# Conditioned two-layer transformer on one core: the values of loop one behind a step's energies, a bias behind the power, and the junction and the MLP's columns in other slots

## The chip, the cores and the metric

The kernel runs on one core of one Trainium2 chip. A core has a matrix engine (PE, with its weight loads shown apart as PEld), a vector engine (DVE), an activation engine (ACT), a general engine (POOL) and a sync engine (SP) whose queue issues nearly all DMAs of this kernel. Each engine takes its instructions in order. The metric is the device time of one execution in microseconds; less is better.

## The reference

The input is 32 sequences of 128 tokens with 512 features and one condition vector of 512 for each sequence. Two layers follow each other:

```python
# layer 0: 16 heads of 32, softmax after the energies, divided by sqrt(D)
h   = gamma(w) * layernorm(x) + beta(w)
q, k, v = h @ Wqkv.T + bqkv
out = softmax(q k^T) / sqrt(D) @ v;  out = out @ Wp.T + bp
h1  = out + x;   x1 = (gamma(w) * layernorm(h1) + beta(w)) + h1
# layer 1: one head of 512, then an MLP of 4 * 512 with an exact gelu
h   = film(rmsnorm(x1), cond)
x2  = x1 + softmax(Q K^T / sqrt(D)) V @ proj_w + proj_b
out = x2 + gelu(film(rmsnorm(x2), cond) @ mlp_w1 + b1) @ mlp_w2 + b2
```

## The kernel before

Everything is float32. A large product is made of three passes with rounded operands: each operand is split into a high part (rounded by a copy) and a low part (what is left, by a subtraction), and high*high, high*low and low*high are added in PSUM (`mm3`, line 157). So each tensor that goes into a product costs a copy (mostly on ACT) and a subtraction (on DVE or POOL).

The work has three stages. The instructions of PE, DVE, ACT and POOL stand in the order in which the program writes them (`manual_schedule`); the order of SP's DMAs is left to the framework's scheduler, and a DMA in SP's queue that waits for its data or its buffer holds up the DMAs behind it.

**Loop one** (layer 0) has 32 steps. Step s handles four heads of a group of four sequences. On PE it goes through the energies of step s (`pse`, line 526, 16 small matmuls), the queries of step s+1 (`psq`, 12 calls of line 157), five of the twelve calls of the projection of an earlier sequence (`psp`), a transposition of the row maxima (`psm`, line 545, called by `maxima`), the other seven projection calls, the energies again in transposed form with the maxima subtracted (`pst`, lines 556 and 561), the keys of step s+1 (`psk`), the heads' outputs and sums (`pso`, `pss`, lines 581 and 586), and then, after the step's end, the values of a sequence of the next group (`psv`, `values0`). Around them stand:
- DVE: the maxima's reductions (line 538) and their split (539, 540), the un-interleaving copy of a transposed sequence (`merge`, line 395), the statistics and the normalization of the next sequence (`stats`, `norm`, lines 296 to 301 and 374), the low part of a finished sequence (`low`, 425), the projection's sum with its residual (`add`, 625), the second normalization of that (`first` and `second`, 639 and 644), and the division of the heads (593 to 595).
- ACT: the bias of the queries and keys (509), the copy of the transposed maxima `mT` (547), four scalings and one rounding of a sequence (`rest`, lines 412 and 421), a copy that prepares the next sequence's DMA transposition (`halves`, 386), four exponentials (568), and the logarithm and exponential of the heads' sums (591, 592).
- POOL: the bias row that is added to the residual (`End.bias`, line 610, after its load), the power -1/2 of a variance (line 308), the sum with the shift (640), and low parts of weights (855, 858) and of heads' outputs (598).

In steps 0 to 3 there is no projection; steps 28 to 31 have no values left to make, and small products of weights (`psvp`, line 686) stand there between a step's heads and the next step's energies.

**The junction** runs once: eleven products that end loop one's last four projections and begin layer 1 (K and V are three and four streams of group 0). **Loop two** has 8 groups of 4 sequences (g = 0 to 7). For each group the scores (`pss`, line 747) are followed by eight slots u: four K products of the next group, then four V products, with the transposed attention (`psaT`) and the outputs (`pso`, line 805 adds and stores them) between them. `Pipeline` objects place the parts of a sequence's preparation into slots: `pipe` for layer 1, `tokens` for the MLP. A sequence that starts at slot t loads two slots earlier, takes its statistics at t, its normalization and `halves` at t+1, its `merge` and `rest` at t+6. `at` lists the (g, u) at which the MLP's first eight sequences start. `Columns` makes the MLP's right-hand operands of two sequences at a time: three sums (lines 890 to 893, DVE), four rounded copies (`heads`, 905, ACT) and four subtractions (`tails`, line 909, two on POOL and two on DVE). In `mm_tile`, the PSUM pool of the projections and the V products, there are two banks, so a V or a projection waits until the one two before it has been read by DVE (lines 123 and 625).

**The MLP** follows in four parts n of eight sequences; its first half-part starts inside the last group of loop two (`hidden(0, 0)`, seven products around the last attention). `Columns` for parts 1 to 3 are made in the second half of the part before.

Of the kernel before, what the change touches and what calls it, by code (L numbers as in the profile page):

```python
# [16 lines left out]
B, N, D = 32, 128, 512  # L17
# [5 lines left out]
G = 4  # L23
NG = B // G
# [17 lines left out]
def cond_seq_kernel(ctx: ExitStack, tc, x, condT, wcond, w0, w1, wk1, wm1, wm2, cols, rows, out):  # L42
    nc = tc.nc
# [14 lines left out]
    def mm_tile(name):  # L58
        return ps_mm.tile([P, D], FP, tag="mm", name=name)
# [7 lines left out]
    def w_tile(name, dt=FR, shape=(P, KC, D)):  # L67
        return big.tile(list(shape), dt, tag="w", name=name)
# [56 lines left out]
    def w_pair(name):  # L125
        return w_tile(f"{name}h"), w_tile(f"{name}l")
# [17 lines left out]
    def sub(pair, *sl):  # L144
        return tuple(t[(slice(None), *sl)] for t in pair)
# [396 lines left out]
    def maxima(s):  # L542

        ps = e_bank(f"psm{s}")[:, :P]
        nc.tensor.transpose(ps, nmx.rearrange("p r j -> p (r j)"), ident)
        mT[s] = sm.tile([P, P], FR, tag="mT", name=f"mT{s}", bufs=2)
        nc.scalar.copy(mT[s], ps)
# [318 lines left out]
    def a_load(n, h):  # L866

        t = w_tile(f"A{n}{'hl'[h]}").rearrange("p c f -> p (c f)")[:, : NA * 2 * P]
        load(t.bitcast(FP), ad[n % FH, h])
        At.setdefault(n, []).append(t.rearrange("p (c k f) -> p c k f", c=NA, k=2))  # L870

    class Columns:
# [9 lines left out]
        def sums(self):  # L882
            n, i = self.n, self.i
            if i == 0:
                Bt[n] = [w_pair(f"B{n}{nm}") for nm in "xuv"]
                t = w_tile(f"B{n}y")
                Bt[n].append((t[:, :2], t[:, 2:]))
            r1, r2 = self.r
            t = d_tile(f"T{n}_{i}", FP, (P, 2 * KC, P))
            nc.vector.tensor_tensor(t[:, 0:2], r2[:, :2], r1[:, :2], ALU.subtract)  # L890
            nc.vector.tensor_tensor(t[:, 2:4], r2[:, 2:], r2[:, :2], ALU.subtract)
            nc.vector.tensor_tensor(t[:, 4:6], r2[:, 2:], t[:, 0:2], ALU.subtract)
            nc.vector.tensor_tensor(t[:, 6:8], t[:, 4:6], r1[:, 2:], ALU.subtract)
            self.parts = [
                (*(p[:, :, ts(i, P)] for p in pair), src, eng)
                for pair, src, eng in zip(
                    Bt[n],
                    (r1, t[:, :4], t[:, 4:], r2[:, 2:]),
                    (nc.gpsimd, nc.gpsimd, nc.vector, nc.vector),
                )  # L900
            ]

# [346 lines left out]
    with tc.manual_schedule(engines=ordered):  # L1249
        new, end = coming(0), None  # L1250
        staged = None
        for s in range(STEPS):
            q, k = qk0(s + 1) if s + 1 < STEPS else ([], [])
            energies(s)
            if s == 0:
                ready.rest()
                ready = None
            if ready:
                ready.merge()
            if end:  # L1260
                end.bias()
            run(q)
            if s == STEPS - 1:
                staged()
                staged = None
            projection = end.stream() if end else []
            run(projection[:5])
            maxima(s)
            if ready:
                ready.rest()  # L1270
            if new:
                new.stats()
                new.norm()
            if ready:
                ready.low()
            if end:
                run(projection[5:])
                end.add()
                end.first()
            elif staged:  # L1280
                staged()
                staged = None
            wn, wj = divmod(s - W_FIRST, W_STEPS)
            if s in (3, 4):
# [12 lines left out]
            if s == 0:  # L1297
                staged = extras[0]()
            if s < KC:
                split_w(W0["p"], raw["p"], s, nc.gpsimd)  # L1300
            coming_stage = extras[s + 1]() if s + 1 in extras else None
            run(k)
            if s == STEPS - 1:
                K = keys1(0)
                run(K[0])
            heads_out(s)
            ready, new = new, coming(s + 1) if s + 1 < STEPS else None
            end = End(s + 1 - G, s + 1 == STEPS) if s + 1 >= G else None
            if s + G < B:
                run(values0(s + G))  # L1310
            if staged:
                staged()
            staged = coming_stage
            if s == 2:
                later["mods"] = r_tile("mods")
            wn, wj = divmod(s + 1 - W_FIRST, W_STEPS)
            if 0 <= wn < KC and wj == 0:
                weights = Weights(wn)
            if s == STEPS - 2:
                l1_load()  # L1320
# [8 lines left out]
        for slot in (-11, -10):  # L1329
            pipe.made[slot] = begins[slot]()  # L1330
        V = values1(0)
        products = [K[1], K[2], 0, K[3], 1, V[0], 2, V[1], 3, V[2], V[3]]
        for u, stream in enumerate(products):
            pipe.start(u - 11)
            if u == 1:
# [15 lines left out]
            pipe.end(u - 11)  # L1351


        at = [(1, 5), (2, 5), (3, 5), (4, 1), (4, 5), (5, 1), (5, 3), (5, 5)]
        batches = [0, 1, 4, 5, 2, 6, 3, 7]
        columns, COLUMNS = {}, (1, 2, 4, 6)
        tokens = Pipeline(
            {2 * G * g + u: lambda b=b: Turned(2, b) for (g, u), b in zip(at, batches)}
        )
        for g in range(NG - 1):  # L1360
            K, V = keys1(g + 1), values1(g + 1)
            outs = []
            run(scores1(g))
            softmax1(g)
            for u in range(2 * G):
                slot = 2 * G * g + u
                for line in (pipe, tokens):
                    line.start(slot)
                if u - 1 in columns:
                    columns[u - 1].tails()  # L1370
                if u in columns:
                    columns[u].sums()
                if 0 < u <= G:
                    outs.append(Out(g * G + u - 1))
                late = ends[g] if g < G else None
                if late and u == 0:
                    late.take_up()
                if late and u == 2:
                    late.first()
                if late and u == 4:  # L1380
                    late.second()
                run(K[u] if u < G else V[u - G])
                if u == 0:
                    divided1(g)
# [8 lines left out]
                if u in columns:  # L1393
                    columns[u].heads()
                if g == NG - 2:
                    if u + 1 in COLUMNS:
                        columns[u + 1] = Columns(0, COLUMNS.index(u + 1))
                    if u == 6:
                        for h in range(2):
                            a_load(0, h)  # L1400


        g = NG - 1
# [7 lines left out]
        products, started = hidden(0, 0)  # L1411
        for j in range(3):
            run(products[j])
        divided1(g)
        run(products[3])
        turn1(g)
        for o in outs:
            o.bias()
        run(products[4])
        for f in (0, FH):  # L1420
            wb_piece(f)
        for i, o in enumerate(outs):
            run(o.stream())
            if i < 2:
                run(products[5 + i])
        row2 = load(r_tile("row2"), rows[R_B2].partition_broadcast(P))
        for q in (1, 3):
            wb_load(q)
# [74 lines left out]
```

## Time and profile before

| | |
|---|---|
| median of 3 runs (lowest, highest) | 1509.9 us (1506.1, 1510.19) |
| the profiled execution: its own time, its span | 1510.46 us, 1508.5 us |
| PE busy | 1478.3 us, 98% of the span |
| DVE, ACT, POOL busy | 1008.4, 760.5, 499.5 us |
| PE idle, by stretch: up to 120 us, 120 to 580, 580 to 900, after | 9.0, 3.3, 12.7, 0.0 us |

A busy PE is not PE at its peak: matmuls are pipelined, and an instruction that waits in the queue behind its weight load can count as busy. So the distance between the starts of neighbouring instructions is read beside the busy time. A call of line 157 starts 0.227 us after the one before it where nothing is in the way. Loop one lasts from about 62 to 592 us, the junction to 627, loop two to 860, the MLP to the end.

### The profile page before, as it was taken

How to read it: one execution, taken by the hardware profiler on the slowest of the kernel's cores; microseconds unless marked ns; L12 is line 12 of the kernel's file. 1: busy time of each engine (PE TensorE's matmuls, PEld its weight loads, DVE VectorE, ACT ScalarE, POOL GpSimd, SP SyncE). 2: the span in 40 equal slices, each digit the busy share in tenths (PEclk: the TensorE clock that was granted, in tenths of full speed). 3: DMA queues.
4: the chain of work that ended last, by engine and by line, in shares of the span. 5: the costliest groups of instructions: out<-in, count | busy, mean ns of one | idle time of the engine just before them, and what ended most of it. 6: DMA issues, size and time to landing. Idle time of an engine off the chain costs nothing.

```text
span 1508.5 us, 25450 instructions
## 1 busy us (share of the span) xinstructions
PE 1478.3 (98%) x9612; PEld 1155.3 (77%) x9612; DVE 1008.4 (67%) x1793; ACT 760.5 (50%) x1415; POOL 499.5 (33%) x440
## 2 busy tenths in 40 slices
PE   8999999999999999999999899999999999999998
PEld 3767776777777766787887788888888888888887
DVE  4656777777777667889997776665557555754342
ACT  1455655566555444666786354535454345523331
POOL 1213554445453243466555422230014000340000
PEclk9999999999999999999999999999999999999999
DMA  8245465664655335788885877937776666934550
GB/s 312 85 151 157 125 198 176 188 190 134 178 152 175 111 115 178 193 209 225 233 214 173 356 238 236 307 132 209 225 266 208 194 203 219 326 122 134 184 173 29
DMA packets 226578, 287.85 MB, mean 191 GB/s; under 512 B 107252, under 2 KB 138100, under 8 KB 224024
## 3 DMA queue, kind: packets, MB, share of 16 engines
q1 hardware_dynamic: 225448, 278.89, 59.8%
q10 hardware_dynamic: 1008, 7.34, 1.4%
q8 instruction: 75, 1.23, 0.3%
q14 instruction: 47, 0.39, 0.1%
HBM read 194.23 MB, written 72.55 MB: 177 GB/s over the span
## 4 chain that ended last, share of the span: by engine, by line
PE 81%; DVE 11%; ACT 3%; issue 2%; POOL 1%; DMA 1%; SPq 0%; POOLq 0%; DVEq 0%; ACTq 0%
PE acc L981 23%; PE psh L157 20%; PE psk L157 6%; PE psv L157 5%; PE psq L157 5%; PE psp L157 5%; PE psV L157 2%; PE pse L526 2%; PE pst L561 2%; PE pso L581 2%; PE pss L586 2%; PE psT L157 1%; DVE tn L395 1%; PE pss L747 1%; DVE stn L296 1%
## 5 line engine op out<-in xcount | busy, mean ns | idle before, releaser
L308 POOL TENSOR_TENSOR rn<-vn,neghalf 128x1 f32<-128x1 f32 x96 | 61.6, 642 | 438.9 <-DVE vn L306 336.6
L386 ACT COPY tn<-x 128x1024 uint16<-128x1024 uint16 x90 | 94.0, 1045 | 60.5 <-DVE x L372 48.4
L919 ACT ACTIVATE c<-c,col 128x512 f32<-128x512 f32 x64 | 46.4, 725 | 141.2 <-DVE c L944 86.0
L538 DVE TENSOR_REDUCE nm<-pse 128x4 f32<-128x512 f32 x128 | 79.4, 682 | 19.4 <-PE pse L526 19.4
L997 POOL TENSOR_TENSOR xe<-xe,row 128x512 f32<-128x512 f32 x32 | 46.5, 1484 | 123.8 <-DMA xe<-xs 123.7
L934 DVE TENSOR_TENSOR c<-psh,ca 128x512 f32<-128x512 f32 x32 | 22.1, 692 | 89.9 <-PE psh L157 84.3
L395 DVE COPY tn<-tn 128x1024 uint16<-128x1024 uint16 x90 | 77.0, 855 | 1.0 <-DMA tn<-tn 1.0
L644 DVE SCALAR_TENSOR_TENSOR xe<-te,re,xe 128x512 f32<-128x512 f32 x28 | 41.1, 1467 | 47.4 <-POOL xe L640 47.4
L296 DVE BATCH_NORM_STATS2 stn<-x 128x6 f32<-128x512 f32 x96 | 65.4, 682 | 5.3 <-DMA x<-in_x 5.2
L568 ACT ACTIVATE e<-pst 128x512 f32<-128x512 f32 x128 | 65.8, 599 | 2.6 <-PE pst L561 2.5
L412 ACT ACTIVATE tn<-tn,mods 128x128 f32<-128x128 f32 x128 | 52.5, 481 | 19.0 <-DVE tn L395 19.0
L308 POOL TENSOR_TENSOR re<-ve,neghalf 128x1 f32<-128x1 f32 x32 | 30.9, 966 | 88.7 <-DVE ve L301 88.7
L372 DVE TENSOR_SCALAR x<-x,rn 128x512 f32<-128x512 f32 x64 | 52.9, 827 | 10.1 <-POOL rn L308 9.0
L610 POOL TENSOR_TENSOR xe<-xe,row 128x512 f32<-128x512 f32 x32 | 42.3, 1323 | 47.7 <-DMA xe<-in_x 46.8
L509 ACT ACTIVATE qk<-psq,col 128x512 f32<-128x512 f32 x32 | 22.1, 690 | 69.7 <-PE psq L157 63.5
L947 DVE TENSOR_TENSOR ca<-psh,ca 128x512 f32<-128x512 f32 x32 | 22.1, 691 | 41.5 <-PE psh L157 41.5
L561 PE MATMUL pst<-qk 32*128 32x128 f32 x1024 | 46.2, 295 | 0.0
L798 POOL TENSOR_TENSOR xe<-xe,row 128x512 f32<-128x512 f32 x32 | 45.8, 1444 | 1.1 <-DMA xe<-xs 1.1
L919 ACT ACTIVATE cb<-cb,col 128x512 f32<-128x512 f32 x32 | 23.2, 725 | 43.1 <-DVE cb L948 43.1
L526 PEld LDWEIGHTS pse<-qk 32*128 32x128 f32 x1024 | 32.1, 186 | 14.2 <-issue 12.7
L412 ACT ACTIVATE tn<-tn,mod 128x128 f32<-128x128 f32 x104 | 42.9, 485 | 0.0
L593 DVE TENSOR_TENSOR pss<-pss,rs 128x512 f32<-128x512 f32 x32 | 22.3, 697 | 29.9 <-ACT rs L592 29.8
(1388 smaller groups left out, 4846.5 us busy)
## 6 DMA issues: line engine op xcount, KB each, us to landing
mod<-mod SPq DMA_DIRECT2D x34, 512.0 KB, 5.4
x<-xs SPq DMA_DIRECT2D x64, 256.0 KB, 3.8
xe<-xs SPq DMA_DIRECT2D x64, 256.0 KB, 3.2
ur<-ud SPq DMA_DIRECT2D x64, 256.0 KB, 4.2
xs<-xe SPq DMA_DIRECT2D x60, 256.0 KB, 2.6
x<-in_x SPq DMA_DIRECT2D x32, 256.0 KB, 3.8
xe<-in_x SPq DMA_DIRECT2D x32, 256.0 KB, 4.3
scw<-scw SPq DMA_DIRECT2D x32, 256.0 KB, 4.7
```

Source lines behind the costliest of these rows:

```text
L157: nc.tensor.matmul(st["ps"], *calls[j], start=(j == 0), stop=(j == n - 1))
L296: nc.vector.bn_stats(st, t)
L308: nc.gpsimd.tensor_tensor(r, v, neghalf, ALU.pow)
L386: nc.scalar.copy(halves.rearrange("p (e d) -> p e d", e=2), X.bitcast(U16).rearrange("p (d e) -> p e d", e=2),)
L395: nc.vector.tensor_copy(self.a.bitcast(U16).rearrange("p (f e) -> p e f", e=2), self.t.bitcast(U16).rearrange("p (e f) -> p e f", e=2),)
L412: nc.scalar.activation(dst[:, c], self.a[:, ts(c, P)], AF.Identity, bias=m[:, q + B : q + B + 1], scale=m[:, q : q + 1],)
L526: nc.tensor.matmul(banks[r][:, ts(i, P)], q[32 * r : 32 * r + 32, ts(i, P)], k[32 * r : 32 * r + 32, ts(i, P)], start=True, stop=True,)
L538: nc.vector.tensor_reduce(nm[:, r], chunks(banks[r]), AX.X, ALU.max, negate=True)
L561: nc.tensor.matmul(banks[r][:, ts(i, P)], k[rr, ts(i, P)], q[rr, ts(i, P)], start=False, stop=True,)
L568: nc.scalar.activation(e, banks[r], AF.Exp)
L919: nc.scalar.activation(t[nm], t[nm], AF.Gelu, bias=col[:, C_B1 + f : C_B1 + f + 1], scale=1.0)
L981: nc.tensor.matmul(accs[i], u[pa][:, ts(i, P)], wb[f // 4][pb][:, f % 4, :], start=(first and j == 0), stop=(last and j == len(PARTS) - 1),)
```

## The change

Five places are edited; what is computed stays the same.

- In loop one the values of step s+3 move from the end of step s-1 (before the energies of step s) to behind the energies of step s. The bias of the residual (`End.bias`, POOL) moves from before the queries to behind the next sequence's statistics and normalization, and so behind their power on POOL. Of the projection's twelve calls nine instead of five stand before the maxima, three behind. And `ready.rest()` (ACT, lines 412 and 421) is now called before `maxima(s)`, so that ACT copies `mT` after it, and not before.
- In the junction the third K stream moves before the first projection, and from there on projections and V streams alternate.
- In loop two the starts of the MLP's sequences move to a start every four slots (slots 13, 17, ... 41 instead of 13, 21, 29, 33, 37, 41, 43, 45), and the first four `Columns` to slots 48, 50, 52 and 53 (before 49, 50, 52 and 54), with their loads two slots ahead instead of one.
- All four subtractions of `Columns` go to DVE, in all four parts of the MLP.
- In the last group, one more MLP product stands before the transposition of the attention.

```diff
-                    (nc.gpsimd, nc.gpsimd, nc.vector, nc.vector),
+                    (nc.vector,) * 4,
...
-            if end:
-                end.bias()
+            if 0 < s <= B - G:
+                run(values0(s - 1 + G))
             run(q)
...
-            run(projection[:5])
-            maxima(s)
+            run(projection[:9])
             if ready:
                 ready.rest()
+            maxima(s)
             if new:
                 new.stats()
                 new.norm()
+            if end:
+                end.bias()
             if ready:
                 ready.low()
             if end:
-                run(projection[5:])
+                run(projection[9:])
...
-            if s + G < B:
-                run(values0(s + G))
...
-        products = [K[1], K[2], 0, K[3], 1, V[0], 2, V[1], 3, V[2], V[3]]
+        products = [K[1], K[2], K[3], 0, V[0], 1, V[1], 2, V[2], 3, V[3]]
...
-        at = [(1, 5), (2, 5), (3, 5), (4, 1), (4, 5), (5, 1), (5, 3), (5, 5)]
+        at = [(1, 5), (2, 1), (2, 5), (3, 1), (3, 5), (4, 1), (4, 5), (5, 1)]
...
-        columns, COLUMNS = {}, (1, 2, 4, 6)
+        columns, FIRST = {}, 2 * G * (NG - 2)
+        columns_at = {FIRST + u: i for i, u in enumerate((0, 2, 4, 5))}
...
-        run(products[3])
+        for j in (3, 4):
+            run(products[j])
         turn1(g)
         for o in outs:
             o.bias()
-        run(products[4])
+        run(products[5])
...
-            if i < 2:
-                run(products[5 + i])
+            if i == 0:
+                run(products[6])
```

More of the change, by code (lines that the diff above doesn't have):

```diff
@@ L1368, in cond_seq_kernel @@
                     line.start(slot)
[L1369 to L1372, printed above, removed]
+                if slot - 1 in columns:
+                    columns[slot - 1].tails()
+                if slot in columns:
+                    columns[slot].sums()
                 if 0 < u <= G:
@@ L1392, in cond_seq_kernel @@
                     line.end(slot)
[L1393 to L1400, printed above, removed]
+                if slot in columns:
+                    columns[slot].heads()
+                if slot + 2 in columns_at:
+                    columns[slot + 2] = Columns(0, columns_at[slot + 2])
+                if slot == FIRST + 6:
+                    for h in range(2):
+                        a_load(0, h)
         g = NG - 1
```

## The prediction

> **What bounds the kernel now.** I read the page first, then PE's waits, then timelines of the places where PE's starts stand apart.
>
> ```profile
> span 1508.5 us, 25450 instructions
> PE 1478.3 (98%) x9612; PEld 1155.3 (77%) x9612; DVE 1008.4 (67%) x1793; ACT 760.5 (50%) x1415; POOL 499.5 (33%) x440
> PE 81%; DVE 11%; ACT 3%; issue 2%; POOL 1%; DMA 1%; SPq 0%; POOLq 0%; DVEq 0%; ACTq 0%
> ...
> PE psV L157 <- DVE V L123: 8.4, 7, 4.9
> PE psp L157 <- DVE xe L625: 1.8, 1, 1.8
> ```
>
> (The last two are PE's waits: total, times, longest.) PE bounds the kernel; no matmul is removed, so the change can win only stalls and transitions, and lose by new stalls. Next a quiet step of loop one (step 21, period 16.23 us), timelines of PE, ACT and DVE:
>
> ```profile
> 416.23 0.39 PE L157 MATMUL psp<-w0ph,o4h 128*128 128x512 f32 x1
> 419.19 0.34 PE L556 MATMUL pst<-mT,pick 32*128 32x128 f32 x4
> ...
> 416.43 0.69 ACT L509 ACTIVATE qk<-psq,col 128x512 f32<-128x512 f32 x1 [2.38 <-PE psq L157]
> 417.68 0.27 ACT L547 CAST mT<-psm 128x128 fp32r<-128x128 f32 x1 [0.56 <-PE psm L545]
> 417.84 1.65 ACT L412 ACTIVATE tn<-tn,mod 128x128 f32<-128x128 f32 x4
> 419.52 0.62 ACT L421 CAST n_24h<-tn 128x512 fp32r<-128x512 f32 x1
> ...
> 416.29 0.75 DVE L395 COPY tn<-tn 128x1024 uint16<-128x1024 uint16 x1
> ```
>
> The projection starts 0.2 us before ACT takes the queries' bias; `mT` is ready 1.2 us before pst needs it. Step 8, where the step takes 18.41 us:
>
> ```profile
> 201.70 1.29 POOL L610 TENSOR_TENSOR xe<-xe,row 128x512 f32<-128x512 f32 x1 [5.44 <-DMA xe<-in_x]
> 202.95 0.55 POOL L308 TENSOR_TENSOR rn<-vn,neghalf 128x1 f32<-128x1 f32 x1
> ...
> 204.11 1.05 ACT L386 COPY tn<-x 128x1024 uint16<-128x1024 uint16 x1 [2.70 <-DVE x L374]
> ...
> 205.71 2.41 PE L581 MATMUL pso<-e,v 128*32 128x128 f32 x31 [0.67 <-ACT e L568]
> ```
>
> A late load holds the bias, this the power behind it on POOL, this DVE's normalization, this ACT's copy and the exponentials behind it, and these PE. Last, group 6 of loop two, and the junction:
>
> ```profile
> 820.95 1.51 DVE L890 TENSOR_TENSOR T<-hT,hT 128x256 f32<-128x256 f32 x1
> ...
> 822.14 1.47 POOL L909 TENSOR_TENSOR B0xl<-hT,B0xh 128x512 fp32r<-128x512 f32 x1
> ...
> 832.70 0.79 PE L157 MATMUL psV<-w1vph,n_28h 128*128 128x512 f32 x1 [4.90 <-DVE V L123]
> 833.29 0.63 PE L157 MATMUL psV<-w1vpl,n_28h 128*128 128x512 f32 x1
> ...
> 611.61 0.50 PE L157 MATMUL psp<-w0ph,o7h 128*128 128x512 f32 x1 [1.80 <-DVE xe L625]
> 613.60 0.63 PE L157 MATMUL psp<-w0pl,o7h 128*128 128x512 f32 x1
> ```
>
> While POOL subtracts, DVE's 0.42 us sums take 1.51; DVE then reaches a V's low part late, PE waits 4.9 us, and afterwards its calls stand 0.43 instead of 0.227 us apart.
>
> **The change, part by part.**
>
> *Quiet steps.* ACT's order becomes queries' bias, four scalings, rounding, `mT`. With p the projection's start: the bias starts p+0.20; back-to-back ACT rows overlap by about 0.11, so the scalings start p+0.77, the rounding p+2.45, `mT` p+2.98 to 3.25, and pst p+3.30 (step 0 shows 0.05 from `mT` to pst). Now pst is at p+2.96: a loss of 0.34. The scalings need the merge. From the heads' end h, the last row of DVE's division ends h+3.5; the reductions, now without a wait for the energies (0.56), take 2.48, the split 0.35, the merge 0.75, so it ends h+7.05, and ACT is ready at about h+7.4: 0.35 to spare. Against the loss: energies no longer cut the stretch of long matmuls. Starts 0.32 instead of 0.227 into them and 0.34 after them go: 0.19. What energies cost right behind the sums (`pss`) no row shows; pso to pss suggests -0.1 to +0.1 of a change, and a gain can't be excluded; I take 0. Net +0.15 (bounds -0.1 to +0.35) in 23 steps (5 to 26, 28): **+3.5** (-2.3 to +8).
>
> *Bias behind the power.* The starts of the energies give steps of 18.41 (8), 18.50 (10), 17.47 (14), 17.11 (11), 16.63 (13), 16.57 (18) against 16.23: 7.3 us over, and ten others 1.1 together, mostly where the bias on POOL stretched line 539 or 540 (0.17) to 0.9 to 1.2. All go except that in 8, 10 and 14 the projection's sum (625) is late next: its chain to the end of line 644 takes 5.9 us, so the division and the merge slip by 0.55, of which 0.35 is covered: 0.2 each. **-7.8** (-8.4 to -5). What the bias meets instead is the normalization (374), 0.55 now; line 372 took 1.51 where a bias started just before it. Then `halves` starts at p+3.5 and ends p+4.6, the exponentials need pst's end at p+4.9: covered; without that cover up to 1 us a step, inside rival B. The sum 625 comes at p+4.2 instead of 4.55, so line 644 is no later.
>
> *Other steps.* In 29 and 30 a `psvp` stands before the energies, DVE splits it first and the merge ends 5.29 after the energies' start: scalings 5.32, pst 7.85 instead of 6.91: 0.94 each, and 0.26 in 31 (pst 7.62): **+2.1** (0 to +2.8). Step 1 has no projection; pst is at p+1.4, and becomes p+3.30: **+1.9** (1.5 to 3.6). Steps 2 to 4 have other PE work there and gain the transitions (0.6); step 27 has no `rest` and loses its late maxima (0.6) and a transition (0.2): **-1.4** (-2 to 0).
>
> *Junction.* It holds 4.2 us of stalls. V streams between projections give each bank one stream more, but every bias now stands behind a power of its own slot, the first also behind `low`. From the rows: power of sequence 7 at 607.2, bias 607.8 to 609.0, sum 609.7, while the second projection could start at 606.5: a 3.2 us wait; then small ones, end at 628 instead of 627. **+1** (-3 to +4.7, with the clock).
>
> *Groups 2 to 4.* Each of groups 2 and 3 gets one more start and merge: statistics 1.23, normalization 0.48, merge 0.75 on DVE, which is busy 28.0 of their 30.5 us already (PE's own work is 28.4). The start fits into a gap of 1.1; the normalization pushes V's low part by 0.55, the merge the next softmax (slack 0.7) by 0.1 to 0.7. 0.55 + 1.2 + 0.6: **+2.4** (0 to +6, both bounds from DVE's sum, idle or not). Tokens leave group 5 and 6: ACT's and DVE's merges at slots 49 and 51 go. Loads on SP follow with two slots of lead.
>
> *Group 6.* It lasts 36.37 us; groups without stalls 28.4 to 28.65. With POOL quiet but for four biases, DVE has 16.4 us for columns (four sums of 0.42, subtractions of 0.68 and 0.42) and 8.2 for the rest: 24.6. Its worst backlog stands at slots 53 and 54, where V's low part is just in time; with biases 0.5 late. 29.0: **-7.4** (-8 to -5).
>
> *Last group.* PE waits 1.69 for the divided attention; one product (1.36) covers most and the biases on POOL, earlier now, no longer stretch line 761 (1.22): -1.8. But A0l stands on SP behind the store of the third output (its sum about 25.7 into group 6) and took 6.7 to land; needed at 32.4: +1. **-0.8** (-1.85 to +1).
>
> *The MLP.* 24 subtractions of 0.68 move to DVE, 176 of 350 us busy from 1160 on, beside PE with no idle after 900: 0 (to +1; DVE would have to be late by a stream of 2.7 us).
>
> Sum: 3.5 - 7.8 + 2.1 + 1.9 - 1.4 + 1 + 2.4 - 7.4 - 0.8 = -6.5; the profiled execution took 1510.46 (0.56 above the median), so 1504.0.
>
> *The clock.* Granted clock 0.5 follows the wait of 1.80 us at 611.6 (for 3.41 us, 1.7 lost) but not the one of 1.69. [...]
>
> **Rivals.**
> - B, the copied maxima bind loop one: slower. Place: reductions, merge, scalings, rounding, `mT`, pst, back to the heads. It decides once the merge is over 0.35 later than I have it, or energies behind pss save nothing. For it: no wait covers `mT` any more. Against: the reductions lose their 0.56 wait. At +0.65 a step instead of 0.15: 23 x 0.5 = 11.5 more, 1515.5.
> - C, DVE takes it all back: groups 2 and 3 are DVE-bound, two starved V's bring the clock down, the junction waits. Groups +6, junction +4.5, group 6 only -6: 1512 at worst, 1509 likely.
> - D, energies behind the heads are nearly free and the junction's alternation works: steps -0.1 (-5.8), junction -2.5 (-3.5 against mine): 1495 to 1498.
>
> **How the numbers follow.** 0.3% (4.5 us) is about what a measurement here can tell from no change; the bound is 1505.4 to 1514.4. Mine 0.55 (1500 to 1509; 0.40 faster, 0.15 same), B 0.14 (0.12 slower, 0.02 same), C 0.16 (0.13 same, 0.03 slower), D 0.15 faster: faster 0.55, same 0.30, slower 0.15. Range 1497 to 1512.5: leaves out half of D's lower end and most of B.
>
> **What would show it.** Quiet steps near 16.4, pst starting just after `mT` behind line 421; steps 8, 10, 14 within 0.3 of the others, line 374 near 1.5; group 6 below 30.5 with line 890 at 0.42; groups 2 and 3 at 31 to 33; a wait of psp for DVE's line 625 at the junction. Wrong if quiet steps leave 16.1 to 16.6, or if PE's clock falls in loop one.

## The result and the profile after

The changed kernel takes 1521.1 us (median of 6 runs, 1518.4 to 1524.0) against 1509.3 for the kernel before (6 runs beside them, 1505.2 to 1511.0). The ratio is 1.0084, 95% interval 1.0064 to 1.0104: slower by 0.8%, where 1504.0 was predicted and 1512.5 was the upper end of the range. The profiled execution took 1519.41 us with a span of 1517.6.

The first page lines of the kernel after, the busy time of each engine and the shares of the chain that ended last:

```profile
span 1517.6 us, 25448 instructions
PE 1470.5 (97%) x9612; PEld 1156.5 (76%) x9612; DVE 1021.5 (67%) x1825; ACT 763.3 (50%) x1415; POOL 449.2 (30%) x408
PE 72%; DVE 14%; ACT 6%; issue 3%; DMA 3%; POOL 2%; SPq 0%; DVEq 0%; POOLq 0%; ACTq 0%
```

PE does the same 9612 products, its share of the chain fell from 81% to 72%, POOL is lighter by 50 us and DVE heavier by 13. PE's waits (total, times, longest) name where the time went:

```profile
PE pst L556 <- ACT mT L547: 15.3, 28, 2.2
PE psV L157 <- DVE V L123: 7.4, 5, 4.7
PE psp L157 <- DVE xe L625: 3.6, 2, 2.5
PE psh L157 <- DVE ca L951: 3.6, 1, 3.6
...
PE psaT L785 <- ACT B0y L905: 2.8, 1, 2.8
```

The first stood once before (0.8 us in step 0) and now stands all over loop one; the fourth, at the MLP's start, and the fifth, in group 6, are new; the second existed before, but its longest moved from group 6 to group 3. The starts of the stages, from both traces, give where the 9.2 us between the spans (1508.48 and 1517.64) lie:

| stretch | before | after | difference | predicted |
|---|---|---|---|---|
| loop one, first to last energies | 516.13 | 517.03 | +0.90 | -1.7, with the line below |
| last energies to layer 1's first K | 9.16 | 9.38 | +0.22 | |
| junction, to the scores of group 0 | 39.64 | 40.96 | +1.32 | +1 |
| groups 0, 1 and 5 | 87.41 | 87.37 | -0.04 | 0 |
| groups 2, 3, 4 | 90.85 | 95.79 | +4.94 | +2.4 |
| group 6 | 36.37 | 33.34 | -3.03 | -7.4 |
| scores of the last group to the end | 666.88 | 671.76 | +4.88 | -0.8 |

A quiet step of loop one in the kernel after (step 21, 16.36 us), timelines of PE, ACT, DVE and POOL:

```profile
417.76 0.33 PE L556 MATMUL pst<-mT,pick 32*128 32x128 f32 x4 [0.28 <-ACT mT L547]
...
415.25 1.64 ACT L412 ACTIVATE tn<-tn,mod 128x128 f32<-128x128 f32 x4
416.92 0.62 ACT L421 CAST n_24h<-tn 128x512 fp32r<-128x512 f32 x1
417.45 0.26 ACT L547 CAST mT<-psm 128x128 fp32r<-128x128 f32 x1
...
416.47 1.50 DVE L374 TENSOR_SCALAR x<-x,mvn,rn 128x512 f32<-128x512 f32 x1 [0.66 <-POOL rn L308]
...
416.40 1.28 POOL L610 TENSOR_TENSOR xe<-xe,row 128x512 f32<-128x512 f32 x1
```

This is as predicted: pst starts right behind `mT`, which stands behind the rounding; the bias meets the normalization (1.50 instead of 0.55 us).

Group 6, where slot 48 now makes its column sums; timelines of DVE, ACT and PE:

```profile
817.39 1.22 DVE L761 TENSOR_TENSOR nm<-usn,nm 128x4 f32<-128x4 f32 x1
...
818.72 1.55 DVE L890 TENSOR_TENSOR T<-hT,hT 128x256 f32<-128x256 f32 x1
...
821.63 1.48 DVE L892 TENSOR_TENSOR T<-hT,T 128x256 f32<-128x256 f32 x1
823.14 0.42 DVE L893 TENSOR_TENSOR T<-T,hT 128x256 f32<-128x256 f32 x1
823.49 0.17 DVE L775 RECIPROCAL inv<-total 128x4 f32<-128x4 f32 x1
823.69 0.69 DVE L776 TENSOR_TENSOR e<-e,inv 128x512 f32<-128x512 f32 x1
...
824.13 0.40 ACT L905 CAST B0y<-hT 128x256 fp32r<-128x256 f32 x1
...
824.53 1.06 PE L785 MATMUL psaT<-ident,e 128*128 128x128 f32 x4 [2.80 <-ACT B0y L905]
```

The sums (0.42 us when POOL is quiet, as line 893 shows) stand between the softmax and the division of the attention (775 and 776) on DVE, and POOL's seven biases (line 798, 813.6 to 822.8) stretch three of them to 1.5. The row of `psaT` names ACT's last copy, which ends at the same moment; but `psaT` starts 0.15 us after the end of the division (824.38), and 0.14 after it in a kernel below where those copies come later, so the division is what PE waits for. The three biases beside the sums take 4.13 us, 1.38 each, hardly more than the 1.28 of a bias in loop one, while each of the three sums takes 1.5 instead of 0.42, 1.1 us longer: nearly all of the lost time stands in DVE's rows.

At the MLP's start (DVE and PE):

```profile
885.11 0.74 DVE L395 COPY tn<-tn 128x1024 uint16<-128x1024 uint16 x1 [7.10 <-DMA tn<-tn]
885.74 0.68 DVE L951 TENSOR_TENSOR ca<-psh,ca 128x512 f32<-128x512 f32 x1
...
886.47 0.79 PE L157 MATMUL psh<-B0vh,A2h 128*128 128x512 f32 x1 [3.56 <-DVE ca L951]
```

DVE waits 7.1 us for a transposition that a merge needs, and the sum of the seventh product, for which PE waits, stands behind the merge. In the kernel before the same merge waited too, and PE did not:

```profile
875.99 0.75 DVE L395 COPY tn<-tn 128x1024 uint16<-128x1024 uint16 x1 [1.05 <-DMA tn<-tn]
```

### The profile page after: what moved, and what is told of

It reads as the page before. It is cut to its first block, busy times and chain, and to the rows that moved or that the text cites. A ratio compares the mean times of both kernels' runs of the same rounds, so it can differ in the third digit from the quotient of the medians.

```text
span 1517.6 us, 25448 instructions
## 1 busy us (share of the span) xinstructions
PE 1470.5 (97%) x9612; PEld 1156.5 (76%) x9612; DVE 1021.5 (67%) x1825; ACT 763.3 (50%) x1415; POOL 449.2 (30%) x408
## 4 chain that ended last, share of the span: by engine, by line
PE 72%; DVE 14%; ACT 6%; issue 3%; DMA 3%; POOL 2%; SPq 0%; DVEq 0%; POOLq 0%; ACTq 0%
PE acc L981 21%; PE psh L157 19%; PE psk L157 6%; PE psv L157 5%; PE psq L157 5%; ACT tn L412 3%; PE pst L561 2%; PE pso L581 2%; PE psV L157 2%; PE pse L526 2%; DVE tn L395 2%; PE pss L586 2%; DVE stn L296 1%; PE psT L157 1%; DVE x L372 1%
## 5 line engine op out<-in xcount | busy, mean ns | idle before, releaser
L997 POOL TENSOR_TENSOR xe<-xe,row 128x512 f32<-128x512 f32 x32 | 44.3, 1410 | 191.8 <-DMA xe<-xs 175.7
L556 PE MATMUL pst<-mT,pick 32*128 32x128 f32 x512 | 40.5, 306 | 15.3 <-ACT mT L547 15.3
L798 POOL TENSOR_TENSOR xe<-xe,row 128x512 f32<-128x512 f32 x32 | 45.3, 1434 | 15.9 <-DMA xe<-xs 15.9
L556 PEld LDWEIGHTS pst<-mT,pick 32*128 32x128 f32 x512 | 25.0, 186 | 29.1 <-ACT mT L547 29.0
L374 DVE TENSOR_SCALAR x<-x,mvn,rn 128x512 f32<-128x512 f32 x26 | 35.2, 1352 | 17.6 <-POOL rn L308 17.6
```

The costliest lines, as they stand in the source:

```text
L556: nc.tensor.matmul(banks[r][:, ts(i, P)], pick[rr, i], mT[s][rr], start=True, stop=False)
```

## The experiments

"From psh to the end" is the time from the first product of the MLP to the end of the span (663.39 before, 668.27 after); the length of a group is that between the starts of two scores.

**Which half lost it.** First the four edits of loop one alone:

```diff
-            if end:
-                end.bias()
+            if 0 < s <= B - G:
+                run(values0(s - 1 + G))
             run(q)
...
-            run(projection[:5])
-            maxima(s)
+            run(projection[:9])
             if ready:
                 ready.rest()
+            maxima(s)
...
+            if end:
+                end.bias()
...
-            if s + G < B:
-                run(values0(s + G))
```

> Only the four edits of loop one (values, bias, the nine projection calls, scalings ahead of the maxima's copy); junction, loop two, columns and last group as before. Theory S (the loss lies in the second half): a quiet step of 16.38 us, layer 1's first K after loop one starts 1.7 us later than before, loop two and the MLP's start as before: +1 to +3 us, 1510 to 1513. Rival L (loop one's new order is the loss, and loop two's new stalls only follow from its shifted transfers): 1516 to 1521, with stalls of 3 to 5 us in loop two here too.

Measured: 1509.7 against 1510.0, ratio 1.0010 (0.9997 to 1.0023). The quiet steps take 16.34 to 16.40, the first to the last energies 519.29 us (516.13 before), and from the first K to the end nothing is lost. Of the 3.2 us, step 1 has 2.9 (a wait of 2.16 us and a half clock behind it, which the profile of after does not have). The profiled execution (1507.9) is not longer than that of the kernel before all the same, as it came to its first energies 3.7 us earlier (58.30 instead of 62.04 us after its start); the kernel after, with the same four edits, has 62.01 there. Theory S holds: these four edits lose nothing behind loop one.

Then all the other edits without these:

```diff
-        products = [K[1], K[2], 0, K[3], 1, V[0], 2, V[1], 3, V[2], V[3]]
+        products = [K[1], K[2], K[3], 0, V[0], 1, V[1], 2, V[2], 3, V[3]]
...
-        at = [(1, 5), (2, 5), (3, 5), (4, 1), (4, 5), (5, 1), (5, 3), (5, 5)]
+        at = [(1, 5), (2, 1), (2, 5), (3, 1), (3, 5), (4, 1), (4, 5), (5, 1)]
...
+        columns_at = {FIRST + u: i for i, u in enumerate((0, 2, 4, 5))}
...
-                    (nc.gpsimd, nc.gpsimd, nc.vector, nc.vector),
+                    (nc.vector,) * 4,
...
-        run(products[3])
+        for j in (3, 4):
+            run(products[j])
...
```

> Everything but loop one's four edits: junction, starts of the MLP's sequences, columns, subtractions on DVE, last group. Theory S: the stalls of group 3 (4.7), group 6 (2.8) and the MLP's start (3.6), each with half a clock for 3.4 us, are here too: group 6 3 us shorter, group 3 about 4.5 longer, the stretch behind the last scores about 5 longer: +6 to +8, 1516 to 1518. Rival L: the stalls come with loop one's shift and go here: group 6 alone is left, 1503 to 1508.

Measured: 1518.8, ratio 1.0068 (1.0050 to 1.0085); group 3 takes 36.01, group 6 33.35, and from psh to the end 667.65. All three stalls are there without any shift of loop one. The loss lies in these edits; rival L falls.

**The order of ACT in loop one.** The first kernel of this section without one of its four edits:

```diff
-            if ready:
-                ready.rest()
             maxima(s)
+            if ready:
+                ready.rest()
```

> The same without one edit: the scalings stand behind the maxima's copy again, as before the change. Theory S with the copy as the binding link of a quiet step: the copy is ready by itself, the 0.28 us wait of pst goes and steps take 16.05 to 16.15; steps 10, 11, 13 and 15 lose their waits of 0.5 to 1.6 too; layer 1's first K 6 to 10 us earlier than in the kernel with all four edits, time 1501 to 1506. Rival: the energies behind the sums, with the values behind them, make the maxima themselves late, whatever ACT does first: steps stay at 16.3 to 16.4 and the time within 2 us of the kernel with all four edits.

Measured: 1505.7, ratio 0.9968 (0.9953 to 0.9983): faster than the kernel before. First to last energies 512.33, 7.0 less than with the scalings first; the waits of pst for `mT` are gone but for step 0. Of the 7.0, step 1 gives 3.2 (its 2.16 us wait and the half clock behind it), steps 29 and 30 1.2, steps 10 to 15 3.0 and step 26 0.7, while steps 8 and 27 lose 0.9 and 1.1; the quiet steps 16 to 25 give only 0.05 each (16.30 to 16.32). The medians differ by 4.0 only: four kernels with the scalings first have the half clock of step 1 in their profile (17.9 us), three do not (16.34 to 16.40). The quiet steps are now held by something else. ACT and PE of that kernel in step 14, which takes 16.30 like them, then DVE and ACT in step 11, which takes 16.86:

```profile
297.00 1.04 ACT L386 COPY tn<-x 128x1024 uint16<-128x1024 uint16 x1
297.95 2.05 ACT L568 ACTIVATE e<-pst 128x512 f32<-128x512 f32 x4
...
300.84 0.27 PE L581 MATMUL pso<-e,v 128*32 128x128 f32 x1
```

```profile
245.78 1.49 DVE L374 TENSOR_SCALAR x<-x,mvn,rn 128x512 f32<-128x512 f32 x1 [0.67 <-POOL rn L308]
...
247.31 1.05 ACT L386 COPY tn<-x 128x1024 uint16<-128x1024 uint16 x1 [0.40 <-DVE x L374]
```

pst has ended at 296.8, but the copy of line 386 stands ahead of the exponentials, so that the last one comes late and the last output product (`pso`) slips in between the sums. Step 26, which has no such copy, takes 15.98. In step 11 the copy starts 0.53 us later in the step than in a quiet one (11.95 instead of 11.42 us after the first energies), behind a normalization that the bias beside it stretches to 1.49, and the step is 0.56 longer.

**Line 386 behind the exponentials.** (With the subtractions on DVE too, which is the next experiment; the base is that kernel.)

```diff
-            if new:
-                new.halves()
             exponentials(s)
+            if new:
+                new.halves()
```

> The same, and in loop one the copy that prepares the next sequence's transposition (line 386) stands behind the four exponentials on ACT instead of ahead of them. Theory E (with the maxima's copy first, the steps' remaining excess is the last exponential: the outputs wait for it 0.1 to 0.25 us in a quiet step and up to 0.9 in steps 8, 11, 13 and 15, where a normalization stretched by the bias holds that copy): quiet steps 16.04 to 16.15 instead of 16.30, steps 8 to 15 within 0.4 of them, 5 to 8 us faster than the kernel without this edit. Rival: the transposition goes out 3 us later, lands behind its place and the merge is late: steps of 16.3 or more, no gain or a loss.

Measured: 1520.8, ratio 1.0075 (1.0058 to 1.0092), against 1504.7 without this edit. (The profiled execution, 1512.8, was the fastest, so its rows hold half of the loss.) Undisturbed steps do take 15.98 to 16.12 (5 to 8, 16 to 18, 20, 22, 23, 25, 26), as theory E says, but steps 9 to 13 take 18.0 to 19.7 and others 16.8 to 17.4. In step 11 the timelines of ACT, PE and SP show:

```profile
245.18 0.62 ACT L597 CAST o2h<-rs 128x512 fp32r<-128x512 f32 x1 [6.92 <-DVE rs L595]
...
246.33 0.50 PE L157 MATMUL psp<-w0ph,o1h 128*128 128x512 f32 x1 [2.33 <-ACT v L493]
...
241.41 0.32 SPq L645 DMA_DIRECT2D xs<-xe  x1
241.82 1.30 SPq L390 DMA_TRANSPOSE tn<-tn  x1
```

The later transposition queues on SP behind a store that waits for line 644, and the next load behind the transposition; DVE's division comes late, and the values' copy, which stands behind the heads' rounding on ACT, holds the bank that the projection needs. Both theories had a part of it: an undisturbed step takes about 16.05, and with this order of the loads too many steps are disturbed.

**The bias alone.**

```diff
-            if end:
-                end.bias()
             run(q)
...
                 new.norm()
+            if end:
+                end.bias()
```

> One edit of loop one alone: the bias of the residual behind the power. By the prediction's term -7.8 us: steps 8, 10, 14, 11, 13 and 18 lose 7.3 us of their excess, 1501 to 1504. Rival (what the changed kernel shows in steps 10, 11, 13 and 15, 4 us over in all): the late load only hands its wait to the projection's sum and through DVE to the next step, and half of the gain goes: -3 to -4, 1505 to 1507.

Measured: 1506.9, ratio 0.9984 (0.9972 to 0.9996). Step 8 falls from 18.41 to 16.23 and step 18 from 16.57 to 16.22, but 10 stays at 18.44 (18.50) and 14 at 17.41 (17.47), and steps 9, 12, 13, 15, 29 and 30 become 0.2 to 0.6 longer (12: 16.79 instead of 16.23); first to last energies 513.93, 2.2 less instead of 7.8. The rival is right in its size, not in its cause. Step 10 on DVE in the kernel before, and then in this one on DVE and POOL, with SP's queue ahead of it:

```profile
235.25 0.69 DVE L296 BATCH_NORM_STATS2 stn<-x 128x6 f32<-128x512 f32 x1 [2.15 <-DMA x<-in_x]
...
238.39 0.55 DVE L374 TENSOR_SCALAR x<-x,mvn,rn 128x512 f32<-128x512 f32 x1 [2.04 <-POOL rn L308]
```

```profile
231.98 0.70 DVE L296 BATCH_NORM_STATS2 stn<-x 128x6 f32<-128x512 f32 x1 [2.50 <-DMA x<-in_x]
...
233.75 1.50 DVE L374 TENSOR_SCALAR x<-x,mvn,rn 128x512 f32<-128x512 f32 x1 [0.66 <-POOL rn L308]
...
233.68 1.29 POOL L610 TENSOR_TENSOR xe<-xe,row 128x512 f32<-128x512 f32 x1
...
223.30 0.34 SPq L645 DMA_DIRECT2D xs<-xe  x1
...
225.70 0.94 SPq L86 DMA_DIRECT2D x<-in_x  x1
```

The sequence's own load `x` is late as well as the one that the bias waits for. Both queue behind the store of line 645, and the statistics waited for `x` in the kernel before already. The edit lets the normalization start 1.02 us earlier in the step (9.03 instead of 10.05 us after the first energies). But the bias now starts beside it and stretches it from 0.55 to 1.50 us, so that it ends at 10.53 instead of 10.60, and the copy of line 386 and the exponentials behind it come no earlier. In step 12 it starts 0.31 us earlier and ends 0.62 later. A quiet step covers the longer normalization (it stays at 16.22); in step 8 the bias's load comes after the power, and the normalization keeps its 0.55. No run has the bias behind the normalization.

**Group 3.** Two edits of the changed kernel's starts, one slot earlier, and back to those of before:

```diff
-        at = [(1, 5), (2, 1), (2, 5), (3, 1), (3, 5), (4, 1), (4, 5), (5, 1)]
+        at = [(1, 5), (2, 0), (2, 5), (3, 0), (3, 5), (4, 0), (4, 5), (5, 0)]
```

> The changed kernel with the MLP's new starts one slot earlier ((2,0), (3,0), (4,0), (5,0) instead of (.,1)): as many statistics, merges and scalings on DVE and ACT in each group. Theory H (the divided attention's tile aT of group 3 gets the buffer of an MLP sequence whose store hTd was issued 5 us before and holds ACT 2.7 us; V's low part is late by that): the store goes out a slot (3.6 us) earlier, ACT does not wait, group 3 takes 30.5 to 31.5 us instead of 35.05, no half clock at its end. Rival D (DVE's sum of work makes group 3 late, as the prediction counted): 34 to 35 again.

```diff
-        at = [(1, 5), (2, 1), (2, 5), (3, 1), (3, 5), (4, 1), (4, 5), (5, 1)]
+        at = [(1, 5), (2, 5), (3, 5), (4, 1), (4, 5), (5, 1), (5, 3), (5, 5)]
```

> The changed kernel with the starts of the MLP's sequences of before. Both H and D: groups 2 and 3 as before, 30.5 each (-0.5 and -4.5). Group 6 gets the merges of slots 49 and 51 back: 33.3 if its stall is the columns' place alone, up to 36 if DVE's sum counts there. Behind the last scores as in the changed kernel (the loads' order is the changed one). 1515 to 1518 against 1519 to 1521.

Measured: one slot earlier 1524.1 (ratio 1.0103, 1.0073 to 1.0132), groups 2 and 3 32.60 and 34.70; the old starts 1514.8 (1.0041, 1.0021 to 1.0061), 30.49 and 30.49, with group 6 at 34.93, between the two lengths expected. So it is the new starts that lengthen groups 2 and 3. With the starts one slot earlier ACT has no wait of `aT` for a store any more, which was this in the kernel after:

```profile
ACT aT L122 <- DMA hTd<-tn: 2.7, 1, 2.7
```

but group 3 is hardly shorter (34.70 instead of 35.05) and group 2 is longer. Theory H falls as the cause of the length: it names only where the stall showed. What stays in each is DVE's work. The columns of these rows are the window, its length, busy time and instructions of PE, PEld, DVE, ACT and POOL, granted clock, DMA share and GB/s; groups 2 and 3 of before, of after, and of the starts one slot earlier:

```profile
685.72:716.23 30.51, 29.16 (x146) 24.08 (x145) 28.02 (x59) 21.80 (x47) 18.30 (x17) 1.00 0.86 233
716.23:746.75 30.52, 29.16 (x145) 24.07 (x144) 28.05 (x59) 21.79 (x47) 18.30 (x17) 1.00 0.90 244
```

```profile
688.10:719.16 31.06, 29.15 (x145) 24.08 (x144) 29.58 (x64) 22.82 (x48) 19.32 (x18) 1.00 0.95 243
719.16:754.21 35.05, 30.31 (x146) 25.07 (x144) 30.91 (x68) 25.26 (x54) 19.23 (x19) 0.95 0.91 236
```

```profile
690.03:722.63 32.60, 29.20 (x146) 24.00 (x144) 30.19 (x66) 23.21 (x49) 18.50 (x18) 1.00 0.86 225
722.63:757.33 34.70, 30.55 (x146) 25.19 (x145) 31.88 (x66) 24.52 (x53) 20.64 (x19) 0.95 0.90 237
```

DVE's busy time in the two groups goes up by 4.42 us (after) and 6.00 (one slot earlier); the two groups take 5.08 and 6.27 longer, about 1.7 of it in each by the half clock at the end of group 3 (3.41 us at 0.5). So rival D holds as to the length. That DVE's work makes it is argued from these sums: they agree over the two groups together and not in each (group 2 of after has 1.56 us more work and is 0.55 longer, group 3 2.86 and 4.53). How much of the 4.5 us of group 3 belongs to the wait of `aT` and how much to the sum was not separated.

**Group 6.** The changed kernel with the columns' slots of before:

```diff
-        columns, FIRST = {}, 2 * G * (NG - 2)
-        columns_at = {FIRST + u: i for i, u in enumerate((0, 2, 4, 5))}
+        columns, COLUMNS = {}, (1, 2, 4, 6)
...
```

> The changed kernel with the columns at slots 49, 50, 52 and 54 as before, all subtractions on DVE. Theory C (in the changed kernel the sums of slot 48 stand between the softmax and the division of the attention on DVE, under POOL's biases, and their copies ahead of psT's on ACT): the wait of 2.8 us and the half clock behind it go, group 6 takes 28.7 to 29.7 us instead of 33.33. Rival: POOL's biases stretch whatever DVE has there, 32 to 33.5. A3h and A3l stand behind the outputs' stores in this kernel: behind the last scores 5 us late as in the changed kernel, or more.

Measured: 1515.4 (1.0048, 1.0026 to 1.0070), group 6 30.17 at full clock. Theory C is right to within half a microsecond. DVE and PE in that kernel:

```profile
821.95 0.18 DVE L775 RECIPROCAL inv<-total 128x4 f32<-128x4 f32 x1 [1.64 <-ACT e L766]
...
823.23 0.41 DVE L890 TENSOR_TENSOR T<-hT,hT 128x256 f32<-128x256 f32 x1
...
823.45 0.63 PE L785 MATMUL psaT<-ident,e 128*128 128x128 f32 x4 [1.43 <-DVE e L776]
```

The sums stand behind the division, and POOL's biases are over by then (at 822.8). From psh to the end it takes 664.81, so the expected 5 us there did not come, which points at the next question.

And the other way round, the subtractions on DVE with the old slots and starts, on top of the loop with the maxima first:

```diff
-                    (nc.gpsimd, nc.gpsimd, nc.vector, nc.vector),
+                    (nc.vector,) * 4,
```

> Loop one as in the kernel with the maxima's copy first (values behind the energies, bias behind the power, nine calls, scalings behind the copy), and all four subtractions of the columns on DVE; junction, starts, the columns' slots and the last group as before. Against the kernel with the maxima first alone, 1505.7. Theory C (group 6 was held by POOL's subtractions alone; DVE's sum there is 24.6 us for the columns and the slots plus 2.5 for the two merges of the MLP's sequences): group 6 takes 30 to 31.5 us instead of 35.83, no half clock there, 1500 to 1501.5. Rival (DVE binds group 6 as it bound group 3, where 28 us of work filled 30.5): 33 to 34.5, 1503 to 1504.5. The MLP behind it: no change by the 24 subtractions.

Measured: 1504.7, ratio 0.9957 (0.9937 to 0.9977). Group 6 takes 30.40 instead of 35.83, as theory C said; but the time fell by only 1 us instead of 4 to 6, because from psh to the end it now takes 667.22 instead of 662.46. Of the edits behind loop one, this one alone gives more than the changed kernel's whole gain in group 6, and something at the MLP's start takes nearly all of it.

**The MLP's start.** The changed kernel with the last group's products as before:

```diff
-        for j in (3, 4):
-            run(products[j])
+        run(products[3])
         turn1(g)
...
-        run(products[5])
+        run(products[4])
...
-            if i == 0:
-                run(products[6])
+            if i < 2:
+                run(products[5 + i])
```

> The changed kernel with the products of the last group in the order of before. On SP the load of A3l (896 KB) then stands ahead of the outputs' stores again, as before, and not ahead of the first transposition of the MLP's ninth sequence. Theory Q (that order makes the transposition land 11.6 us after its issue, DVE's merge wait 7.1 and PE 3.6, with half a clock): from the MLP's first product to the end 663 to 664 us instead of 668.3, 1514 to 1516. Rival: the transposition is late since group 6's loads moved: 667 to 669 again.

Measured: 1520.0 (1.0075, 1.0046 to 1.0104), from psh to the end 664.11. That stretch is as theory Q expected; the time isn't, as this execution lost 1.9 us more in loop one and 2.2 more up to the last scores, by half clocks in step 1 and at the junction that the profile of after has not. And Q isn't the cause: the kernel with the old starts keeps the changed order of the loads and takes 663.47. What differs is when the merge's transposition lands, and what stands behind it:

| kernel | merge starts, us after the last scores' start | PE's wait there | from psh to the end |
|---|---|---|---|
| before | 34.4 | none | 663.39 |
| after | 39.2 | 3.56 | 668.27 |
| old starts | 36.3 | 0.47 | 663.47 |
| old columns | 37.2 | 1.37 | 664.81 |
| old last group | 37.0 | 2.13 | 664.11 |
| maxima first | 35.5 | none | 662.46 |
| subtractions on DVE | 38.5 | 2.49 | 667.22 |

The view of the tile `tn` of the kernel after, from 855 to 890 us, gives the time from issue to landing of its three transfers; the longest is the transposition issued at 873.5, which lands at 885.1 (in the kernel before the longest took 8.8):

```profile
DMA to landing us min/median/max: 7.5/7.6/11.6
```

Ahead of it in SP's order stand two pieces of the MLP's first operand for each half-part (896 KB each), pieces of the second operand and the outputs' stores. The test moves the merge, not the transfers:

```diff
-                if j == 5 and fp:
-                    state[fp - 1].merge()
                 if j == 6 and fp:
+                    state[fp - 1].merge()
                     state[fp - 1].rest()
```

> The changed kernel with one more edit: in the MLP the merge of the next part's sequence (DVE, line 395) stands behind the seventh product of a half-part instead of behind the sixth. Theory M (the stall at the MLP's start is this merge: its transposition lands 39.2 us after the last scores begin, behind 13 us of queued loads, and the sums of the seventh product stand behind it on DVE): PE's wait of 3.6 us at line 951 and the half clock behind it go although the transposition lands as late; from the MLP's first product to the end 663 to 664.5 us instead of 668.3, the time 1515.5 to 1517.5 against 1521.1. Rival (the loads themselves bind there, PE meets them a product later): 667 to 669.

Measured: 1515.7, ratio 1.0040 (1.0025 to 1.0055), 5.5 us less than the changed kernel. From psh to the end 663.98. On DVE:

```profile
877.52 0.68 DVE L951 TENSOR_TENSOR ca<-psh,ca 128x512 f32<-128x512 f32 x1
884.04 0.76 DVE L395 COPY tn<-tn 128x1024 uint16<-128x1024 uint16 x1 [5.24 <-DMA tn<-tn]
```

The transposition lands as late as in the changed kernel (38.6 us after the last scores' start), DVE still waits 5.2 us for it, and PE no longer does. Theory M is shown; that the loads as such bind falls.

**A version that beats both**: the loop with the maxima first, the subtractions on DVE and the later merge, all else as before.

> Values behind the energies, bias behind the power, nine calls, scalings behind the maxima's copy, subtractions on DVE, the merge behind the seventh product; junction, starts, columns and last group as before. Theory M: the kernel without the later merge gave 5.4 us in group 6 and lost 4.8 at the MLP's start; that loss goes, 1499.5 to 1502 against 1504.7 without this edit and 1510 before. Rival (the loads bind): 1503.5 to 1506.

Measured: 1502.0 (1498.0 to 1503.4), ratio 0.9947 (0.9933 to 0.9960): 0.5% faster than the kernel before. It stands at the upper end of what theory M gave: from psh to the end 665.02, so 2.2 of the 4.8 us came back. The MLP's first product now waits 1.24 us for A0l (0.47 in the kernel with the subtractions on DVE, nothing before), and a product of line 981 waits 1.01 us for DVE's line 1001, 294 us after the last scores' start. Both kernels with the later merge have this last wait, and no other has it.

## Why the prediction was wrong

By its own terms, from the profiled executions (9.2 against -6.5, 15.7 apart: 5.7 at the last group and the MLP, 4.4 in group 6, 2.8 in loop one, 2.5 in groups 2 to 4, 0.3 at the junction):

- **Quiet steps, +0.15 each: right**, parts included. They take 16.34 to 16.40 (+0.11 to +0.17), pst starts behind `mT` as drawn, line 374 takes 1.50, and the energies right behind the sums cost nothing: undisturbed steps of the kernel with line 386 moved take 15.98 to 16.12, around the 16.04 that 16.23 less the 0.19 of the transitions gives.
- **Bias behind the power, -7.8: failed.** The step was "All go except that in 8, 10 and 14 the projection's sum (625) is late next", and of the normalization that it is "covered". That holds in a quiet step. In steps 10, 12 and 14 the sequence's own load is late too (the kernel before has the wait, 2.15 us in step 10, and the prediction shows step 8 alone). Nothing covers the normalization there, and the bias beside it takes 0.95 of the 1.02 us back in step 10. Alone, the edit gives 2.2 us in loop one. In the changed kernel steps 5 to 26 together take 0.7 us less, where this term and the quiet steps gave 4.5. There the rest of the lateness meets `mT` behind the scalings, and steps 11, 13 and 15 take 17.71, 17.33 and 17.65 (16.86, 17.08 and 17.07 with the maxima first). This is rival B's mechanism, in a few steps instead of in all.
- **Other steps, +2.1, +1.9, -1.4: right.** Steps 29 and 30 lose 0.93 each (0.94 predicted), step 1 1.4 (1.9; 2.9 in the kernels where a half clock follows its wait), steps 2 to 4 gain 1.4 (0.6 predicted), step 27 0.6 (0.8). With the bias's term loop one comes out at +1.1 instead of -1.7.
- **Junction, +1: right,** +1.3; the wait is 2.48 instead of 3.2. With a half clock (five other kernels with this junction) it is +2.5 to +3.8, and +2.3 in the sixth without one, all inside the bounds; that the profiled kernel came so near is luck of the phase (its wait falls on two stretches of the clock's grid, last section).
- **Groups 2 to 4, +2.4: mis-sized,** +4.9, inside its bounds (0 to +6). The step "The start fits into a gap of 1.1" was wrong: a gap on an engine that works 28.0 of 30.5 us was the time of its own waits. Over groups 2 and 3, 4.4 us more of DVE's work came with 5.1 us more of length, of which a half clock has 1.7.
- **Group 6, -7.4: failed,** -3.0, outside its bounds (-8 to -5). The step compared DVE's sum (24.6 us, about right: 24.7 with the old slots) with PE's and looked at the order in slots 53 and 54 alone: the first columns were moved to slot 48, where they stand between two links of the attention's chain, under POOL's biases, seven and not "four biases". With the columns back in their old slots the group takes 30.17 instead of 33.33.
- **Last group and MLP, -0.8 and 0: failed,** +4.9. The term looked at A0l alone and called the rest covered ("beside PE with no idle after 900"). Between 860 and 890 DVE's order holds a merge that needs a transposition, which queues behind loads and stores. In the kernel before it was 1.05 us late, which the profile showed. A shorter group 6 uncovers it: the subtractions on DVE make the group 5.4 us shorter, and the merge then starts 38.5 instead of 35.5 us after the last scores' start. Of the last group's -1.8, the wait of 1.69 us went, and one of 0.93 us for ACT's `aT` came.

The rivals: C ("DVE takes it all back") names two of the three places, and its price (1512 at worst) was too low, since it left group 6 at -6 and the MLP at 0. None of the cases had the transfers of the MLP's start, which alone are 4.3 of the 8.6 us by which the range ended too early (what the later merge gave back from psh to the end).

## What to carry to other kernels

Before a gain is booked, look at the first place behind it where an engine waits for a transfer by a microsecond that costs nothing yet: a gain upstream turns it into the next stall, and here a merge moved by one product gave 5 us back. A sum of busy times says whether an engine can do its work, not whether it does it in time: read which instruction stands ahead of a chain's next link in the new order, and what POOL does beside it just then (here DVE's sums took 1.5 us instead of 0.42 beside its biases). When a wait is to go, ask of its neighbours whether they wait for the same queue, and what the moved instruction will run beside.

## What the runs showed of the hardware that was not expected

The clock did not follow the length of a wait. In the traces of before and after, from loop one to the last product, the half-clock spells last 3.41 us or twice that and start on a grid of that step (613.05 and 831.50 in the kernel before, 64 steps apart; 746.07, 824.57 and 886.01 in the kernel after, 23 and 18), and what they went with is the work within one stretch of the grid. The kernel before at its wait of 1.80 us, and the one after at its wait of 2.48, in stretches of that grid (columns as above; the first number after the length is PE's busy time, the third from the end the granted clock):

```profile
609.63:613.05 3.42, 1.62 (x7) 1.20 (x7) 3.28 (x9) 1.53 (x2) 0.39 (x2) 1.00 0.85 215
613.05:616.46 3.41, 3.41 (x10) 2.67 (x9) 3.31 (x6) 2.26 (x6) 2.12 (x2) 0.50 0.89 248
```

```profile
606.12:609.53 3.41, 2.20 (x10) 1.50 (x8) 1.88 (x4) 3.36 (x5) 2.58 (x3) 1.00 0.26 51
609.53:612.95 3.42, 2.14 (x9) 1.77 (x10) 2.86 (x6) 1.05 (x1) 0.50 (x1) 1.00 1.09 263
```

The longest wait is split over two stretches, PE works in each for over half of it, and the clock stays. Step 1 shows the same with a wait of 2.16 us: in the kernel with loop one's edits alone it lies in one stretch with 1.26 us of work, and half a clock follows; in the kernel after it is split over two with 2.01 and 2.66 us, and none does. In the traces of before and after, between the same bounds, every stretch at full clock with 1.80 us or more of idle PE (1.80, 2.80, 3.11, and 3.41 in each of the two) was followed by half a clock, and none with 1.40 or less was. So here a wait of about 2 us cost 1.7 more or nothing. Group 6 takes 33.33 with a wait of 2.80 in one stretch and half a clock behind it, and 31.89 at full clock with one of 2.95 (the kernel with the starts one slot earlier; where that wait lies on the grid was not shown).
